# A two-layer graph kernel: the first graph's turn ahead of the score weights, the last graphs turned on TensorE, and both ends of the order placed anew

## The chip, the core and the metric

The kernel runs on one core of one Trainium2 chip. TensorE multiplies matrices, VectorE (DVE) and ScalarE (ACT) read its sums from PSUM, GpSimd (POOL) works on SBUF alone, and SyncE (SP) issues nearly all DMAs from one queue, in order. The metric is the device time of one execution in microseconds. Before the change the median of three runs is 2680.06 us (2679.51 to 2684.79).

## What is computed

128 graphs of 128 nodes with 512 features each pass two layers. Both have a layer norm and a ReLU ahead of them and add their result to the input. The first is graph attention with eight heads, the second a hypergraph convolution with a hidden size of 1024:

```python
h = relu(layernorm(x))
feats = einsum("nf,hfu->hnu", h, W)                      # per head, 64 units
dense = leaky_relu(e_self[:, None] + e_neigh[None, :]) + NEG_BIG * (1 - adj)
x = x + relu(softmax(dense) @ feats + b)                 # layer 0
h = relu(layernorm(x))
conv(v, W, b) = D^-1 H B^-1 H^T (v @ W^T) + b            # H = adj != 0
x = x + conv(layernorm(relu(conv(h, W1, b1))), W2, b2)   # layer 1
```

Everything is float32. `e_self` and `e_neigh` are the features times two vectors per head; the kernel folds these vectors into 16 extra columns of the first weight, the score weights.

## The kernel before

Work goes graph by graph, and two graphs make a pair. Of each graph there are steps with names: `x` loads, normalizes and turns (transposes) the input; `f` is the product with the first weight (eight matmuls, four to each of two PSUM banks, L583; the trace shows every matmul as two records, a transpose as one); `e` and `d` make the scores, which ACT, POOL, DVE and ACT again turn into exponentials `pp`; `p` turns them; `av` multiplies them with the features; `o` turns that result back; then the second norm `h` and the product `z` with the graph's own matrix `kk`. Of each pair there are the products `u1` to `u7` with W1 and `v1` to `v7` with W2, a seven-product scheme (four blocks of weights, two graphs; L830), between which DVE adds up the sums (`.keep` steps), the ReLU `r`, its turn (`ra.turn`, `rb.turn` for the first and second graph of the pair), and the last products `ya` and `yb`, after which `finish` (L947) adds the input and sends the result out.

A turn is done in one of two ways (`send` L481, `fetch` L490, `turn` L503). From the fifth graph on, SP writes the rows to DRAM, reads them back in four blocks, and DVE transposes 32x32 blocks. For the first four graphs (`DIRECT = 4`) nothing is sent: TensorE transposes 128x128 blocks, four to a PSUM bank, and DVE (first four blocks) or ACT (next four) copies them out. `blocks` (L475) says how the rows must lie for each way.

PSUM has eight banks. Two form the tile `pa` (first user: the rows of the score weights, then every `f` and half of every `d`), two rotate as `ps` (turns, `e`, `z`, `av`, `y`, biases), and four are named `ux`, `uy`, `vx`, `vy`, for the sums of the pairs' products; `uy` or `vy` also takes a part of `d`.

The order of all work is written out by hand. Every step has a place, a number in microseconds: its graph's origin (19.7 apart, the first eight listed in `EARLY`), plus the step's offset in `AT`, less a correction by group for the first eight graphs (`EARLY`) and the last ones (`LATE`). `put` (L990) works this out, and `Order.issue` sorts by place and issues; each engine then runs its instructions in that order, and waits at each for what it needs. So a place that changes moves a step only if it passes another one of the same engine.

At the start, TensorE spreads the rows `a_self` and `a_neigh` over 128 partitions (`score_rows`, L299, into `pa`); ACT copies the second to SBUF for POOL; DVE and POOL multiply both with the four blocks of the first weight and DVE sums up (`score_weights`, L305: three DVE instructions and one of POOL for each of four blocks). `bias_rows` (L326) spreads `b0`, `b1`, `b2`. `features` (L583) of graph 0 takes the score columns from the separate tile `we_sb`; `join_weights` (L323) copies them into the weight for later graphs.

Of the kernel before, what the change touches and what calls it, by code (L numbers as in the profile page):

```python
# [20 lines left out]
G = 2  # L21
STEP = 19.7
EARLY = (
    (0, 0, 4.32, -3.31, -3.04, -23.63, 1.9, -22.92, -47.35),
    (17.06, 1.25, -1.46, -0.55, 0, 0, -1.12, -1.26, -1.12),
    (36.56, 0, 0, -4.01, -4.09, 17.16, 19.45, 9.03, 5.36),
    (56.46, 0, 24.24, 0, 0.38, 0.45, -2.88, 0.44, 1.71),
    (76.16, 0, 0, 0, 0.74, -35.63, -3.58, -9.83, -12.38),
    (95.86, -1.88, 14.47, -1.29, 0, 0, 0, 0, 0.17),
    (115.56, -1.01, -1.01, -1.1, -1.57, -1, -6.4, -14.14, 11.79),  # L30
    (135.26, 0, 0.2, 0, 0.25, 0, 0, 0, -0.33),
)
LATE = (
    (0, 0.06, 0.98, 0, 13.88, 13.88, 5.19, 7.18),
    (0, -31.07, 0.07, 0.07, 0.26, 0.3, 0.26, -1.16),
    (0, 0, 0.62, 0.51, 4.26, 4.81, 4.81, 4.81),
    (0, 11.83, 0, -0.45, 0.41, -0.45, -0.45, 0.35),
)
AT = {
    "x.load": -21.95,  # L40
    "x.stats": -15.53,
    "x.rstd": -15.44,
    "x.relu": -11.99,
    "x.send": -10.85,
    "x.fetch": -7.73,
    "x.turn": -5.54,
    "f": 0,
    "f.keep": 3.07,
    "e": 3.9,
    "e.keep": 3.95,  # L50
    "d": 5.43,
    "d.leaky": 6.82,
    "d.mask": 8.25,
    "d.max": 12.88,
    "d.exp": 13.13,
    "d.exp1": 15.17,
    "p.send": 18.81,
    "p.fetch": 20.79,
    "p.turn": 26.62,
    "av": 29.32,  # L60
    "av.keep": 29.42,
    "o.send": 30.44,
    "o.fetch": 35.98,
    "o.turn": 37.55,
    "o.scale": 38.14,
    "o.add": 39.38,
    "h.stats": 42.94,
    "h.rstd": 43.02,
    "h.relu": 46.17,
    "z": 48.11,  # L70
    "z.keep": 51.23,
    "h.add": 51.08,
    "mask.load": -38.04,
    "mask": -24.21,
    "adj.load": -17.21,
    "adj.turn": 13.26,
    "adj.weigh": 17.47,
    "k": 31.92,
    "k.keep": 38.55,
    "us1": 55.31,  # L80
    "us2": 57.51,
    "us3": 55.61,
    "us4": 90.08,
    "u1": 62.8,
    "u1.keep": 70.95,
    "u6": 73.82,
    "u6.keep": 81.18,
    "u2": 76.53,
    "u2.keep": 78.64,
    "r.aL": 79.95,  # L90
    "u5": 84.05,
    "u7": 85.22,
    "u7.keep": 85.8,
    "r.bR": 88.18,
    "u4": 90.98,
    "u4.keep": 96.2,
    "r.bL": 96.27,
    "u3": 90.17,
    "u3.keep": 92.36,
    "r.aR": 96.53,  # L100
    "rb.send": 96.52,
    "rb.stats": 100.8,
    "ra.send": 99.31,
    "ra.stats": 103.65,
    "rb.fetch": 97.63,
    "rb.turn": 102.59,
    "ra.fetch": 101.73,
    "ra.turn": 113.63,
    "vs1": 112.91,
    "vs3": 117.27,  # L110
    "vs2": 120.49,
    "vs4": 137.15,
    "v1": 129.15,
    "v1.keep": 132.3,
    "a1": 133.14,
    "b1": 137.57,
    "b0": 137.67,
    "v6": 141.07,
    "v6.keep": 141.58,
    "v2": 136.71,  # L120
    "v2.keep": 138.79,
    "v5": 144.57,
    "v7": 142.41,
    "v7.keep": 145.53,
    "v4": 150.39,
    "v4.keep": 153.91,
    "v3": 150.01,
    "v3.keep": 151.98,
    "ya": 161.01,
    "ya.keep": 163.25,  # L130
    "yb": 178.91,
    "yb.keep": 183.24,
}
W2_AT = (43.52, -5.54, 3.84, 45.52, 47.16, 57.34, 58.49, 1.46, 76.99, 1.07, 11.58, 8.21)
DIRECT = 4


class Order:
# [4 lines left out]
        self.todo = []  # L143

    def at(self, place, fn, *args):
        self.todo.append((place, len(self.todo), fn, args))

    def issue(self):
        for _, _, fn, args in sorted(self.todo, key=lambda t: t[:2]):
# [4 lines left out]
def gat_then_hypergraph_kernel(  # L154
# [17 lines left out]
    N, C, F = x.shape  # L172
# [44 lines left out]
    def load_x(n):  # L217
        S[n]["xt"] = io.tile([P, F], F32, tag="xt", name=f"xt_{n}")
        nc.sync.dma_start(S[n]["xt"], x[n])
# [18 lines left out]

    load_x(0)
    S[0]["done"] = {"x.load"}
    t1, t2, t4 = (const.tile([P, KP, FV], F32, name=f"w2_t{i}") for i in (1, 2, 4))
    gb = const.tile([2 * KH, P], F32, name="gb")
    rows = {}
# [43 lines left out]
    bw_bc = const.tile([P, F], F32, name="bw_bc")  # L289
    cm = const.tile([P, F], F32, name="cm")  # L290
    gbT = const.tile([P, 2 * KH], F32, name="gbT")
    a_ps = psum2("a_bc")
    a_bc = [a_ps[:, t] for t in range(2)]
    an_bc = wk.tile([P, F], F32, tag="h1", name="an_bc", bufs=1)

    def spread(out, row):
# [175 lines left out]

    def blocks(n, rows):  # L475

        if n < DIRECT:
            return rows.rearrange("p (k b y) -> p k b y", b=NB, y=B)
        return rows.rearrange("p (b k y) -> p k b y", b=NB, y=B)

    def send(n, key, rows, k):  # L481

        S[n][key + "r"] = rows
        if n < DIRECT:
            return
        d = dr.tile([P, NB, k * B], F32, tag=key + "d", name=f"{key}d_{n}")
        S[n][key + "d"] = d
        nc.sync.dma_start(d, rows.rearrange("p (b c) -> p b c", b=NB))

    def fetch(n, key, k):  # L490
        if n < DIRECT:
            return
        d = S[n].pop(key + "d")
        m = wk.tile(
            [P, NB, k * B], F32, tag=key + "m", name=f"{key}m_{n}", bufs=1
        )
        S[n][key + "m"] = m
        for b in range(NB):
            nc.sync.dma_start(  # L499
                m[b * B : (b + 1) * B], d[:, b, :].rearrange("(a x) r -> x a r", x=B)  # L500
            )

    def turn(n, key, k, tag, bufs=2):  # L503
        rows = S[n].pop(key + "r")
        S[n][tag] = wk.tile([P, k, P], F32, tag=tag, name=f"{tag}_{n}", bufs=bufs)
        if n < DIRECT:
            for q in range(k // 4):
                t = psum(f"{key}t_{n}_{q}")
                for j in range(4):
                    at = (q * 4 + j) * P  # L510
                    nc.tensor.transpose(t[:, j * P : (j + 1) * P], rows[:, at : at + P], ident)
                half = S[n][tag][:, q * 4 : (q + 1) * 4, :].rearrange("p k c -> p (k c)")
                if q:
                    nc.scalar.copy(half, t)
                else:
                    nc.vector.tensor_copy(half, t)
            return
        nc.vector.transpose(  # L518
            S[n][tag].rearrange("p k (a x) -> p k a x", x=B),
            S[n].pop(key + "m").rearrange("p a (k y) -> p k a y", y=B),  # L520
        )
# [51 lines left out]
    def relu_x(n):  # L573
        s = S[n]
        s["xn"] = wk.tile([P, F], F32, tag="xn", name=f"xn_{n}", bufs=1)
        norm_relu(
            n,
            "a",
            blocks(n, s["xn"]),
            s["xt"].rearrange("p (k b y) -> p k b y", k=KF, y=B),  # L580
        )

# [98 lines left out]
    def exps(n, part):  # L681
        s = S[n]
        if part == 0:
            s["pp"] = wk.tile([P, H * P], F32, tag="pp", name=f"pp_{n}", bufs=1)
            s["rsum"] = sm.tile([P, H], F32, tag="rsum", name=f"rsum_{n}")
        nmx, sc = s["nmx"], s["sc"]
        for h in range(part * H // 2, (part + 1) * H // 2):
            nc.scalar.activation(  # L688
                blocks(n, s["pp"])[:, h],
                sc[:, h, :].rearrange("p (b y) -> p b y", y=B),  # L690
                AF.Exp,
                bias=nmx[:, h : h + 1],
                accum_out=s["rsum"][:, h : h + 1],
            )
# [17 lines left out]
    def keep_attention(n):  # L712
        s = S[n]
        s["oT"] = wk.tile([P, F], F32, tag="oT", name=f"oT_{n}", bufs=1)
        nc.scalar.activation(
            blocks(n, s["oT"]),
            s.pop("av").rearrange("p (k b y) -> p k b y", k=KF, y=B),
            AF.Relu,
        )
# [44 lines left out]
    def keep_hidden(n, q, hid):  # L764

        s = S[n]
        if "r" not in s:
            s["r"] = wk.tile([P, DH], F32, tag="r", name=f"r_{n}")
            s["sum"] = sm.tile([P, 2], F32, tag="sum", name=f"sum_{n}")
        nc.scalar.activation(  # L770
            blocks(n, s["r"])[:, q * 4 : (q + 1) * 4],
            hid.rearrange("p (k b y) -> p k b y", k=4, y=B),
            AF.Relu,
            accum_out=s["sum"][:, q : q + 1],
        )
# [186 lines left out]


    order = Order()
    order.at(-30, score_rows)
    for k in range(KF):
        order.at(-40 + k, load_w0, k)
        order.at(-12 + k, score_weights, k)
    order.at(-12, bias_rows, "b0", b0_bc)
    order.at(-30, load_mask, 0)  # L970
    order.at(0.5, join_weights)
    order.at(2, load_w1)
    order.at(W2_AT[0], load_w2)
    order.at(W2_AT[1], bias_rows, "b1", b1_bc)
    order.at(W2_AT[2], bias_rows, "b2", b2_bc)
# [168 lines left out]
    for n in range(N):  # L1144
        if n % G == 0:
            for group, key, fn in first:
                if n or key != "mask.load":
                    put(n, group, AT[key], fn, n // G)
        for group, key, fn in parts:
            if n or key != "x.load":  # L1150
                put(n, group, AT[key], staged, key, fn, n, S)
        if n % G == G - 1:
            for group, key, fn in second:
                put(n, group, AT[key], staged, key, fn, n // G, SP)
# [37 lines left out]
```

## Time and profile before

| | |
|---|---|
| median of three runs | 2680.06 us |
| the profiled execution | 2679.3 us |
| its span, first to last instruction | 2677.5 us |
| TensorE busy | 2612.1 us (98%) |
| VectorE, GpSimd, ScalarE busy | 1909.0, 1878.9, 1502.1 us |
| mean granted TensorE clock | 0.989 |

The profiled execution's own time is 1.8 us more than its span. In the views below a line of the timeline has the start, the time that it took, the engine, the source line, the operation, what it writes and reads, and in brackets the idle time of the engine before it with what ended it. A "PEld" line is a weight load of TensorE. A table by stretches gives, for each stretch of the span, its length and each engine's busy time.

### The profile page before, as it was taken

What the parts mean: (1) busy time and instruction counts of PE and PEld (TensorE: products, weight loads), DVE (VectorE), ACT (ScalarE), POOL (GpSimd) and SP (SyncE); (2) the same over time, 40 slices, a digit from 0 to 9 for tenths busy, and PEclk for the clock granted to TensorE, in tenths of its full rate; (3) what the DMA queues carried; (4) which work ended last, traced back from release to release, by engine and by line L of the source; (5) the groups of instructions that cost most, each with busy time, mean ns of one, the idle gap of its engine ahead of it and who ended that gap; (6) DMA issues with size and microseconds to landing.
All of it is one profiled execution on the core that took longest, in us unless ns stands there. A gap on an engine that the chain in (4) does not pass through costs nothing.

```text
span 2677.5 us, 42248 instructions
## 1 busy us (share of the span) xinstructions
PE 2612.1 (98%) x12433; PEld 1803.4 (67%) x12433; DVE 1909.0 (71%) x3554; ACT 1502.1 (56%) x4945; POOL 1878.9 (70%) x2196
## 2 busy tenths in 40 slices
PE   7799999999999999999999999999999999999998
PEld 4566666676666667667667667667666666667665
DVE  4566777777776777777777777777777677777763
ACT  3466556556556556656656556556556556555542
POOL 4667777777767777767767767777777777777762
PEclk8899999999999999999999999999999999999999
DMA  3246566566666566566666566666666666666632
GB/s 111 65 129 184 177 203 193 176 200 196 181 200 191 176 207 195 185 192 199 184 189 199 180 195 198 186 192 195 189 188 199 184 188 199 191 186 200 193 119 90
DMA packets 504496, 482.18 MB, mean 180 GB/s; under 512 B 136117, under 2 KB 406469, under 8 KB 504266
## 3 DMA queue, kind: packets, MB, share of 16 engines
q1 hardware_dynamic: 504256, 479.47, 59.4%
q8 instruction: 99, 1.62, 0.3%
q14 instruction: 131, 1.07, 0.1%
q10 hardware_dynamic: 10, 0.01, 0.0%
HBM read 250.70 MB, written 228.59 MB: 179 GB/s over the span
## 4 chain that ended last, share of the span: by engine, by line
PE 71%; DMA 11%; SPq 6%; DVE 5%; ACT 4%; issue 2%; POOL 1%; DVEq 0%; ACTq 0%; POOLq 0%
PE f L594 14%; PE uy L852 10%; PE vy L852 8%; PE vx L852 7%; PE uz L852 6%; PE vz L852 6%; PE ux L852 6%; SPq L499 5%; DMA pm<-pd 4%; PE av L704 4%; PE y L943 3%; PE z L744 3%; PE d L655 2%; DMA rd<-r 2%; DMA xm<-xd 2%
## 5 line engine op out<-in xcount | busy, mean ns | idle before, releaser
L594 PE MATMUL f<-w_sb,hT 128*128 128x264 f32 (+1 forms) x2048 | 485.8, 391 | 11.8 <-issue 6.6
L594 PEld LDWEIGHTS f<-w_sb,hT 128*128 128x128 f32 x2048 | 392.9, 193 | 109.3 <-issue 37.4
L688 ACT ACTIVATE pp<-sc,nmx 128x128 f32<-128x128 f32 x1024 | 397.4, 393 | 98.7 <-DVE nmx L679 98.7
L674 POOL TENSOR_TENSOR sc<-sc,at 128x1024 f32<-128x1024 f32 x128 | 303.2, 2368 | 65.6 <-ACT sc L669 65.6
L852 PE MATMUL vx<-w_sb,rT 128*128 128x256 f32 x1024 | 248.2, 385 | 1.0 <-ACT b L906 1.0
L852 PE MATMUL ux<-w_sb,zT 128*128 128x512 f32 x512 | 240.6, 592 | 0.0
L636 ACT COPY lt<-eT 128x128 f32<-128x128 f32 x128 | 34.1, 266 | 364.4 <-PE eT L628 364.4
L459 POOL TENSOR_SCALAR ve_a<-mv_a 128x1 f32<-128x1 f32 x128 | 28.3, 221 | 258.4 <-DVE mv_a L457 240.3
L852 PEld LDWEIGHTS vx<-w_sb,rT 128*128 128x128 f32 x1024 | 184.8, 190 | 34.2 <-issue 13.0
L730 POOL TENSOR_TENSOR xt<-xt,o 128x512 f32<-128x512 f32 x128 | 163.0, 1273 | 51.7 <-DVE o L726 49.8
L688 ACT ACTIVATION_READ_ACCUMULATOR pp<-sc,nmx 128x1 f32 x1024 | 195.9, 191 | 0.0
L518 DVE STREAM_TRANSPOSE pT<-pm 128x1024 f32<-128x1024 f32 x124 | 154.0, 1242 | 52.1 <-DMA pm<-pd 48.6
L787 ACT ACTIVATE sq<-r,nm 128x512 f32<-128x512 f32 x256 | 182.9, 715 | 4.2
L679 DVE TENSOR_REDUCE nmx<-sc 128x8 f32<-128x1024 f32 x128 | 155.4, 1214 | 35.2 <-POOL sc L674 35.0
L770 ACT ACTIVATE r<-aL 128x512 f32<-128x512 f32 x64 | 40.4, 632 | 237.0 <-DVE aL L863 237.0
L762 POOL TENSOR_TENSOR xt<-xt,b_bc 128x512 f32<-128x512 f32 x128 | 163.1, 1274 | 10.0
L828 POOL TENSOR_TENSOR rT<-rT,rT 128x512 f32<-128x512 f32 x64 | 82.0, 1281 | 125.3 <-DVE rT L518 108.3
L469 ACT ACTIVATE h<-xt,nmr_b,rstd_b 128x512 f32<-128x512 f32 x128 | 103.4, 808 | 115.6 <-POOL nmr_b L464 115.6
L761 POOL TENSOR_TENSOR xt<-xt,h 128x512 f32<-128x512 f32 x128 | 163.4, 1277 | 5.5 <-ACT h L469 5.3
L744 PEld LDWEIGHTS z<-kk,h 128*128 128x128 f32 x1024 | 134.2, 193 | 41.9 <-issue 27.4
L852 PEld LDWEIGHTS ux<-w_sb,zT 128*128 128x128 f32 x512 | 97.1, 190 | 94.6 <-issue 78.4
L518 DVE STREAM_TRANSPOSE rT<-rm 128x1024 f32<-128x1024 f32 x124 | 151.5, 1221 | 12.4 <-DMA rm<-rd 12.2
(163 smaller groups left out, 6358.3 us busy)
## 6 DMA issues: line engine op xcount, KB each, us to landing
pd<-pp SPq DMA_DIRECT2D x124, 512.0 KB, 3.7
pm<-pd SPq DMA_DIRECT2D x496, 128.0 KB, 3.7
rd<-r SPq DMA_DIRECT2D x124, 512.0 KB, 3.6
rm<-rd SPq DMA_DIRECT2D x496, 128.0 KB, 3.0
xt<-in_x SPq DMA_DIRECT2D x128, 256.0 KB, 3.0
out<-xt SPq DMA_DIRECT2D x128, 256.0 KB, 2.8
xd<-xn SPq DMA_DIRECT2D x124, 256.0 KB, 2.2
xm<-xd SPq DMA_DIRECT2D x496, 64.0 KB, 2.0
```

The source lines that it names most:

```text
L499: nc.sync.dma_start(m[b * B : (b + 1) * B], d[:, b, :].rearrange("(a x) r -> x a r", x=B))
L518: nc.vector.transpose(S[n][tag].rearrange("p k (a x) -> p k a x", x=B), S[n].pop(key + "m").rearrange("p a (k y) -> p k a y", y=B),)
L594: nc.tensor.matmul(s["f"][:, b, cols], hT[:, k, :], weights[:, k, b, :], start=(k == 0), stop=(k == KF - 1),)
L674: nc.gpsimd.tensor_tensor(s["sc"], s["sc"], neg.to_broadcast([P, H, P]), ALU.add)
L679: nc.vector.tensor_reduce(s["nmx"], s["sc"], AX.X, ALU.max, negate=True)
L688: nc.scalar.activation(blocks(n, s["pp"])[:, h], sc[:, h, :].rearrange("p (b y) -> p b y", y=B), AF.Exp, bias=nmx[:, h : h + 1], accum_out ...
L730: nc.gpsimd.tensor_tensor(s["xt"], s["xt"], s.pop("o").rearrange("p k c -> p (k c)"), ALU.add)
L744: nc.tensor.matmul(s["z"][:, k * P : (k + 1) * P], s["h1"][:, k * P : (k + 1) * P], SP[n // G]["kk"][:, n % G, :], start=True, stop=True,)
L761: nc.gpsimd.tensor_tensor(s["xt"], s["xt"], s["h1"], ALU.add)
L762: nc.gpsimd.tensor_tensor(s["xt"], s["xt"], b2_bc, ALU.add)
L787: nc.scalar.activation(sq, s["r"][:, q * 512 : (q + 1) * 512], AF.Square, bias=nm[:, 1:2], accum_out=ss[:, q : q + 1],)
L852: nc.tensor.matmul(p[w + bank][:, 0:cols], left[:, k, :], right[:, k, :], start=(first and k == 0), stop=(k == kb - 1), skip_group_check=n ...
```

## The change

The change has six parts.

1. The first graph's turn goes ahead of the score weights on DVE, and ahead of the bias rows on TensorE. Its norm goes ahead of the mask on POOL and ahead of the score rows' copy on ACT.
2. The two score rows are spread into the banks `ux` and `vx`, and no longer into `pa`.
3. The rows of `b2` are spread ahead of the first `f`, together with those of `b0` and `b1`. On SP, `x` of graphs 1 and 2 is loaded right after the first weight and mask; the second-layer weight W2 is loaded ahead of the third pair's mask.
4. The last graph's `p` and `o` turns (graph 127) and the last pair's `r` turns (graphs 126 and 127) are done on TensorE: 4 bank fills for `r`, 2 for `p`, 1 for `o`, each of four transposes and a copy.
5. The places of the first eight and now the last six graphs are set anew (`EARLY`, `LATE`).
6. Offsets in `AT` move a little. In every pair of the middle this passes other steps in four places: on TensorE `u6` goes ahead of `v3` and `v4`, and `v6` ahead of `yb`; on POOL `b1` goes ahead of `us2`, and `b0` behind `o.add`; on SP the mask load goes behind the fetch of `ra`. DVE and ACT keep their order in the middle.

At the ends, TensorE's order changes so: after graph 0, `e` 4 goes ahead of `u1` 0, `u6` 0 ahead of `z` 2, `u5` 1 ahead of `e` 7, `av` 6 ahead of `z` 5; in the last pairs `u6` stands ahead of `v3`, `yb` between `v6` and `v7`, the turn `rb` 63 between `v5` and `v3` of pair 62, `ya` 62 between `v1` and `v2` of pair 63. On DVE, `yb.keep` 61 and `v7.keep` 62 stand ahead of the turn `rb` 63, `yb.keep` 60 ahead of the turn `rb` 62, and `yb.keep` 59 and the turn of `p` 127 ahead of the turn `rb` 61. On SP `rb` and `ra` of pairs 61 and 62 are both sent before either is fetched. Counts of instructions in the middle do not change.

The core of the diff (the tables of numbers are cut to what is spoken of):

```diff
 LATE = (
-    (0, 0.06, 0.98, 0, 13.88, 13.88, 5.19, 7.18),
...
+    (0, 0, 0, 0, 0, 43.36, 50.78, 44.34),
+    (0, 0, 0, -1.28, 0, -2.85, 0, -0.14),
...
 )
 AT = {
...
-    "mask.load": -38.04,
-    "mask": -24.21,
+    "mask.load": -34.65,
+    "mask": -21.04,
...
-    "u6": 73.82,
+    "u6": 70.97,
...
-    "b1": 137.57,
-    "b0": 137.67,
+    "b1": 135.65,
+    "b0": 138.73,
...
-    "yb": 178.91,
-    "yb.keep": 183.24,
+    "yb": 180.67,
+    "yb.keep": 182.25,
 }
 DIRECT = 4
+LAST = {"x": 0, "p": 1, "o": 1, "r": 2}
...
-    load_x(0)
-    S[0]["done"] = {"x.load"}
...
-    a_ps = psum2("a_bc")
-    a_bc = [a_ps[:, t] for t in range(2)]
+    a_bc = [psum_sums(tag, f"a_bc_{tag}") for tag in ("ux", "vx")]
...
-    def blocks(n, rows):
+    def direct(n, key):
+        return n < DIRECT or n >= N - LAST[key]
+
+    def blocks(n, key, rows):
-        if n < DIRECT:
+        if direct(n, key):
             return rows.rearrange("p (k b y) -> p k b y", b=NB, y=B)
...
     def turn(n, key, k, tag, bufs=2):
...
-        if n < DIRECT:
+        if direct(n, key):
             for q in range(k // 4):
...
-    order.at(-30, score_rows)
+    order.at(W2_AT[12], score_rows)
     for k in range(KF):
-        order.at(-40 + k, load_w0, k)
-        order.at(-12 + k, score_weights, k)
-    order.at(-12, bias_rows, "b0", b0_bc)
-    order.at(-30, load_mask, 0)
+        order.at(-99 + k, load_w0, k)
+        order.at(W2_AT[13] + k * W2_AT[14], score_weights, k)
+    order.at(W2_AT[15], bias_rows, "b0", b0_bc)
+    order.at(-95, load_mask, 0)
+    order.at(W2_AT[16], adj_masks, 0)
     order.at(0.5, join_weights)
-    order.at(2, load_w1)
+    order.at(W2_AT[17], load_w1)
...
-            if n or key != "x.load":
+            if n < 3 and key == "x.load":
+                order.at(-100 + 6 * n, staged, key, fn, n, S)
+            else:
                 put(n, group, AT[key], staged, key, fn, n, S)
```

## The prediction

> **What bounds the kernel now.** I read the busy shares first, then the table by stretches, then TensorE's timeline at both ends. From the page:
>
> ```profile
> PE   7799999999999999999999999999999999999998
> ...
> PEclk8899999999999999999999999999999999999999
> ```
>
> TensorE is full but for the first three and the last of 40 slices, and only the first two slices show a lower clock. The table by stretches (start, end and length, then busy time of PE, PEld, DVE, ACT, POOL, then clock):
>
> ```profile
> 0.00:21.00 21.00, 9.99 (x15) 3.91 (x15) 10.71 (x28) 4.23 (x6) 7.85 (x16) 1.00 0.80 225
> 21.00:200.00 179.00, 152.21 (x708) 101.51 (x709) 99.48 (x202) 88.28 (x290) 112.98 (x117) 0.87 0.29 87
> 200.00:2560.00 2360.00, 2349.33 (x11331) 1631.56 (x11330) 1748.10 (x3247) 1374.35 (x4544) 1707.88 (x2006) 1.00 0.64 191
> 2560.00:2674.00 114.00, 100.55 (x382) 66.45 (x380) 50.24 (x81) 35.22 (x107) 50.18 (x59) 0.96 0.29 93
> ```
>
> The middle holds 2360 us and only 10.7 us (2360.00 less 2349.33) in which TensorE is idle: two `f` lie 39.74 us apart where nothing waits, 40.0 on average. The ends are small but loose: 11.0 us idle before the first `f` at 21 us, 26.8 to 200 us, 13.4 in the last 114. So what can be won lies at the ends; in the middle the change must only not lose. The start:
>
> ```profile
> 6.47 5.32 PE L297 MATMUL b<-w_t,ones 1*128 1x512 f32 x6
> 9.36 1.10 POOL L527 TENSOR_SCALAR at<-at 128x256 f32<-128x256 f32 x1 [7.98 <-DMA at<-in_adj]
> 13.27 1.08 PE L511 MATMUL xt<-ident,xn 128*128 128x128 f32 x4 [1.48 <-ACT b_bc L331]
> 18.99 1.28 DVE L314 TENSOR_REDUCE we_sb<-prod 128x8 f32<-128x512 f32 x2
> 20.19 0.68 DVE L516 COPY hT<-xt 128x512 f32<-128x512 f32 x1
> 20.97 5.88 PE L594 MATMUL f<-w_sb,hT 128*128 128x256 f32 x16 [6.61 <-issue]
> 28.47 1.12 PE L297 MATMUL b<-w_t,ones 1*128 1x512 f32 x2
> ```
>
> The reader sees graph 0's norm behind the mask on POOL (9.36), its turn on TensorE at 13.27, and the copy that `f` 0 needs (20.19) at the end of the score weights in DVE's queue. "issue" before `f` 0 is that copy. The end (TensorE):
>
> ```profile
> 2587.14 1.98 PE L704 MATMUL av<-pT,feats 128*64 128x128 f32 x16 [4.04 <-DVE pT L518]
> 2589.04 3.56 PE L852 MATMUL vz<-w_sb,rT 128*128 128x256 f32 x8
> ...
> 2620.89 1.97 PE L852 MATMUL vz<-w_sb,rT 128*128 128x256 f32 x8 [2.76 <-DVE v L915]
> ...
> 2642.98 1.99 PE L852 MATMUL vy<-w_sb,rT 128*128 128x256 f32 x8 [0.65 <-DVE a L915]
> ...
> 2649.71 3.22 PE L852 MATMUL vz<-w_sb,rT 128*128 128x256 f32 x8 [3.00 <-DVE v L915]
> ...
> 2658.65 1.99 PE L852 MATMUL vx<-w_sb,rT 128*128 128x256 f32 x8 [0.98 <-ACT b L906]
> ...
> 2663.87 1.99 PE L852 MATMUL vy<-w_sb,rT 128*128 128x256 f32 x8 [0.65 <-DVE a L915]
> ...
> 2668.26 1.97 PE L852 MATMUL vz<-w_sb,rT 128*128 128x256 f32 x8 [0.67 <-DVE v L915]
> ```
>
> `av` 127 waits for a turn through DRAM; `v3` of pairs 61 and 62 waits for `v7.keep`, which stands in DVE's queue behind the turn `rb`, itself waiting for a DMA. And two groups of eight take 3.56 and 3.22 us where the others take 1.97.
>
> **The Trainium skill.** "TensorE: Matmul & The Clock Gate", Part 1: the clock is halved by default and after a window of about 3.4 us without enough activity. The trace agrees: the clock is 0.50 from 2585.41 to 2592.23 and from 2650.26 to 2653.67, right after the two long stalls, and for 47.8 us in all between 32 and 148 us. Part 4 says that transposes don't count as activity; no stretch here shows it alone. "DMA: Bandwidth & Descriptors", Anatomy of one DMA: about 2 us fixed for each; here 2.0 to 3.7 us from issue to landing, twice for a turn. "PSUM — Partial Sum Buffer", on bank collisions: a bank must be guarded as a whole; so while `pa` holds the score rows, `f` 0 would have to wait for their last reader.
>
> **The start, step by step.** `x` 0 lands as before, its sums are ready at 4.46 us; without the mask ahead, POOL's three instructions (1.27 us at 10.54) end at 5.8, ACT's norm (0.81) at 6.6, just as TensorE ends the score rows (6.67). Four transposes (1.08): 7.8; copy (0.68): 8.5. The first weight is there by 8 us (the small packets of its eight DMAs end then). Now four bias spreads stand ahead of `f` 0, not three: 4 x 1.77 (5.32/3) = 7.1, so `f` 0 starts at 14.9, not 20.97. Its score columns need the score weights: DVE from 8.5, four times 2.05 (18.28 to 20.27 for one, say), 16.7; covered by `f` 0's main part (at 5.5 to 5.9 us to about 20.5), the columns (1.85) end at 22.3. Before, 28.54 plus 1.1 for `b2` (28.47), `e` 0 at 29.52; now `e` 0 at 22.5. Gain 7.0. The rest is pushed by `f` 0's end and follows: ACT now runs `e.keep` 0 ahead of graph 1's norm, 0.8 us, hidden while TensorE runs `d` 0 (0.71) and DVE the adjacency (1.6). W1 moves behind two loads of 256 KB; it ended by 17 to 18 us before, and POOL, who now takes a 2.35 us block of it ahead of the mask of scores, needs it at 19. The new banks alone save little: the last reader of the score rows would be done by 15.4, against 14.9.
>
> From graph 3 to 8 swaps on TensorE mostly fill one wait and open another, since DVE, ACT and POOL pace this part (`u6` 0 ahead of `z` 2 fills 1.43 us, but `f` 5 waits for DVE's turn anyway; `u1` 0 behind `e` 4 puts 1.0 us ahead of `d` 4, hidden by POOL's queue; `av` 6 may gain 1.9). I take 0, between -2.5 and +2.
>
> **The end, step by step.** Removed waits, all from the lines above: `av` 127 4.04; at `v3` 61 2.76 less what remains with `u6` (1.73 us) ahead of it and `v7.keep` still behind a DMA, 0.9, so 1.9; `v7` 62 0.65 (`yb`, 0.85, fills it); `v3` 62 3.00 (`v7.keep` no longer stands behind a turn); `v2` 63 0.9; `v3` 63 0.67. Sum 11.1. Added transposes: 28, at 0.5 us for four (groups of four take 0.42 to 0.66 when the clock is full): 3.6. Their seven copies lie on DVE and ACT, which are half idle there. Added waits: `z` 126 for a bank, 0.3; `u7` 62 for `u6.keep`, 0.4; `v1` 63 for the copy of `ra`, 0.25; and `z` 127. Its chain (copy `o`, scale, add, norm, ReLU) took 7.0 us before (2595.23 to 2602.27), just hidden; now `o` is turned earlier, but TensorE arrives 4.9 us earlier: 1.4 open. Sum 2.35. Behind `z` 127 stand `v1` 61 and everything later. The slow clock of 2585 to 2592 cost 0.9 (`av`, 1.98 against 1.10) and 1.6 (`v3`): 2.5, gone with the stall. That of 2650 cost 1.6; eight transposes stand there now, so I leave it in. Sum: -11.1 + 3.6 + 2.35 - 2.5 = -7.65.
>
> **The middle.** No instruction is added. `u6` needs `us2`, done 15 us earlier (1534.3 against about 1549.6), and a bank which ACT left 1.9 us before; `v3` and `v4`, 1.73 us later, are read by DVE 0.8 and 1.6 us after that. `b1` fills a POOL wait of 1.23 us. The mask load (0.40 us on SP) leaves a hole before the fetch of `ra` and now stands ahead of the sends of `y` and `x`; `x.send` waits for ACT anyway (1509.1), and `f` has 1.0 us of slack behind its turn. It also leaves the DMA engines to `p`'s fetch, whose turn causes most of the 10.7 us. I take 0, from -4 to +4.
>
> Sum: -7.0 + 0 - 7.65 + 0 = -14.7. Profiled execution 2679.3 - 14.7 = 2664.6; it lay 0.76 below the median of the runs, so the forecast is 2665.3.
>
> **Rivals.** *One end only* (the start's slow clock windows fall worse, or the transposes keep the clock down at the end and `z` 127 waits 3 us): -7 to -8, 2672.5. For it: 17 us of half clock between 80 and 97. *More*: the second slow window goes too (1.6), the middle's turns lose half their waits (4), graphs 4 to 8 gain 2: 2658. For it: the middle's stalls sit mostly on odd graphs, where the mask load was. *Slower*: the mask load holds `x.send` of odd graphs by 0.4 us, and that comes through to `f` in each of 60 pairs, +24, so 2665.3 + 24 = 2689. It decides once `hT` is late by more than the 1.0 us of slack; `f` waited in only a few odd graphs, by at most 1.05, which speaks against. *Nothing*: the start's gain is swallowed by the pace of DVE and POOL from graph 3 on, and the end's by cold transposes: 2679.
>
> **Chances.** Forecast 0.58, one end 0.17, more 0.13, slower 0.07, nothing 0.05. Range: the forecast's own 2661 to 2670, reaching to the cases beside it: 2656 to 2675. A measurement of this kernel tells about 0.2% (5.4 us) from no change. Faster by more 0.87, within 0.06, slower 0.07.
>
> **What would show it.** `f` 0 starts at 15 us, not 21, and `e` 0 at 22.5; `av` 127 waits under 0.5 us and has no half clock around it; `z` 127 waits 1 to 2 us; `v3` 62 doesn't wait; `f` to `f` stays at 39.74 per pair with about 11 us idle in the middle. The forecast is wrong if the middle's idle time grows beyond 15 us, or if the distance from `f` 0 to `f` 8 (150.4 us) grows by what the start won.

## The result, and the profile after

The changed kernel takes 2672.8 us (median of 20 runs, 2666.6 to 2679.3), the kernel before on the same chip 2680.9 (20 runs, 2677.2 to 2687.2). The ratio is 0.9965, 95% interval [0.9957, 0.9973]: 9.4 us faster by the ratio, 8.2 by the medians, where 14.7 had been forecast. The profiled execution took 2671.9 us, its span is 2670.1. The busy tenths of TensorE look as before but for the first slice (8 for 7) and the last (9 for 8):

```profile
PE   8799999999999999999999999999999999999999
...
PEclk8899999999999999999999999999999999999999
```

The table by stretches of the changed kernel (columns as in the prediction; the first stretch ends at 15 us, where `f` 0 now begins):

```profile
0.00:15.00 15.00, 9.95 (x14) 3.84 (x14) 4.81 (x18) 4.23 (x6) 6.14 (x15) 1.00 0.77 204
15.00:190.00 175.00, 142.59 (x668) 94.88 (x669) 98.01 (x196) 83.28 (x270) 108.95 (x115) 0.86 0.29 88
190.00:2550.00 2360.00, 2348.98 (x11336) 1631.44 (x11335) 1746.32 (x3244) 1374.82 (x4543) 1707.03 (x2005) 1.00 0.64 191
2550.00:2667.00 117.00, 104.49 (x398) 69.42 (x396) 56.94 (x94) 39.74 (x127) 56.77 (x64) 0.96 0.33 105
```

These four lines are those of the kernel before, cut at the new borders. The same cut of the changed kernel:

```profile
0.00:15.00 15.00, 11.96 (x17) 4.33 (x17) 9.12 (x26) 4.33 (x6) 7.84 (x16) 1.00 0.78 205
15.00:190.00 175.00, 146.73 (x706) 98.28 (x706) 99.74 (x203) 87.92 (x289) 111.81 (x117) 0.89 0.32 97
190.00:2550.00 2360.00, 2340.80 (x11284) 1621.68 (x11285) 1737.95 (x3226) 1365.81 (x4521) 1677.12 (x2000) 1.00 0.63 190
2550.00:2667.00 117.00, 111.60 (x464) 75.06 (x460) 60.12 (x102) 42.79 (x132) 58.69 (x65) 1.00 0.24 79
```

Three of the stretches got fuller: TensorE does more in the same time at the start, and the last stretch has full clock (1.00 for 0.96). The third got emptier: 19.2 us idle (2360.00 - 2340.80) where the kernel before had 11.0. That is where part of the gain went. TensorE's timeline at the start of the changed kernel:

```profile
6.79 1.12 PE L514 MATMUL xt<-ident,xn 128*128 128x128 f32 x4 [0.91 <-ACT xn L469]
7.83 7.19 PE L297 MATMUL b<-w_t,ones 1*128 1x512 f32 x8
14.96 6.53 PE L597 MATMUL f<-w_sb,hT 128*128 128x256 f32 x16
21.32 1.85 PE L597 MATMUL f<-we_sb,hT 128*128 128x8 f32 x16
23.52 0.41 PE L631 MATMUL eT<-ident,pad 128*128 128x128 f32 x2 [0.35 <-DVE pad L611]
```

`x` 0 is turned at 6.79 us (13.27 before), the spreads of the biases fill the time to 14.96, and `f` 0 follows with no wait. `f` 8 starts at 161.78 us, 9.6 sooner than before (171.41). The end:

```profile
2585.65 1.13 PE L747 MATMUL z<-kk,h 128*128 128x128 f32 x8 [0.44 <-DVE pT L519]
2586.71 1.09 PE L707 MATMUL av<-pT,feats 128*64 128x128 f32 x16
...
2589.55 1.89 PE L855 MATMUL vz<-w_sb,rT 128*128 128x256 f32 x8
...
2597.60 1.98 PE L855 MATMUL uz<-w_t,us 128*128 128x512 f32 x4 [1.42 <-DVE aL L866]
...
2601.69 1.16 PE L747 MATMUL z<-kk,h 128*128 128x128 f32 x8 [0.39 <-ACT h L469]
...
2643.31 1.92 PE L855 MATMUL vz<-w_sb,rT 128*128 128x256 f32 x8
...
2660.79 1.97 PE L855 MATMUL vz<-w_sb,rT 128*128 128x256 f32 x8 [0.67 <-DVE v L918]
```

`av` 127 (2586.71) no longer waits and takes 1.09 us for 1.98; the two slow groups of eight (3.56 and 3.22) take 1.89 and 1.92. A wait that was not foreseen stands at 2597.60. Followed step by step, the changed kernel is 9.6 us ahead of the kernel before at graph 8, 2.3 us behind it at 2540 to 2580 us, and 7.5 ahead at the last instruction. Both ends gave almost 10; what lies between, for which the forecast had 0, took 12 in this execution: 9.3 in graphs 8 to 119, whose order the experiments put back, and 2.5 from there to `f` 127. Which waits grew there, by group on TensorE from 200 to 2500 us (busy us and mean ns, then the idle time before the group), the kernel before first:

```profile
L594 PE MATMUL f<-w_sb,hT 128*128 128x264 f32 x1840 | 429.0, 386 | 2.6 <-DVE hT L518 2.4
...
L704 PE MATMUL av<-pT,feats 128*64 128x128 f32 x1840 | 125.8, 279 | 7.8 <-DVE pT L518 7.4
```

```profile
L597 PE MATMUL f<-w_sb,hT 128*128 128x264 f32 x1840 | 429.8, 387 | 7.0 <-DVE hT L521 6.8
...
L707 PE MATMUL av<-pT,feats 128*64 128x128 f32 x1824 | 124.7, 279 | 9.3 <-DVE pT L521 9.0
```

The times of the instructions are the same within 1 ns; the waits for the two turns through DRAM grew, `f`'s most. Of the 48 pairs of graphs 12 to 107, 18 keep the undisturbed 39.74 us, where 26 did.

### The profile page after: what moved, and what is told of

The parts are those of the page before. It is cut to its first block, busy times and chain, and to the rows that moved or that the text cites. A ratio compares the mean times of both kernels' runs of the same rounds, so it can differ in the third digit from the quotient of the medians.

```text
span 2670.1 us, 42320 instructions
## 1 busy us (share of the span) xinstructions
PE 2611.1 (98%) x12461; PEld 1799.3 (67%) x12461; DVE 1907.0 (71%) x3554; ACT 1500.8 (56%) x4948; POOL 1855.5 (69%) x2196
## 4 chain that ended last, share of the span: by engine, by line
PE 60%; DMA 17%; SPq 8%; DVE 7%; ACT 5%; issue 2%; POOL 1%; DVEq 0%; ACTq 0%; POOLq 0%
PE f L597 12%; PE uy L855 8%; SPq L502 7%; PE vy L855 7%; PE vx L855 6%; DMA pm<-pd 6%; PE uz L855 5%; PE ux L855 5%; PE vz L855 4%; DMA xd<-xn 3%; PE av L707 3%; PE y L946 3%; DMA pd<-pp 2%; DMA rd<-r 2%; PE z L747 2%
## 5 line engine op out<-in xcount | busy, mean ns | idle before, releaser
L521 DVE STREAM_TRANSPOSE hT<-xm 128x512 f32<-128x512 f32 x124 | 88.0, 710 | 114.7 <-DMA xm<-xd 114.6
L641 DVE TENSOR_TENSOR rt<-diag,eT 128x256 f32<-128x256 f32 x128 | 51.9, 405 | 153.6 <-ACT lt L639 153.6
```

The source lines that it names most:

```text
L521: nc.vector.transpose(S[n][tag].rearrange("p k (a x) -> p k a x", x=B), S[n].pop(key + "m").rearrange("p a (k y) -> p k a y", y=B),)
```

## The experiments

All but one have the changed kernel's code; a table `MID` replaces places of `AT` in graphs 8 to 119 alone, so that the ends keep their order. Each group of four ran on one chip, beside the kernel before; the three groups on three chips, so runs are compared within a group. Runs of different groups are compared only by their ratio to the kernel before beside them. Of each kernel one execution has a trace.

**First group: is it the order of the middle?** The kernel before took 2672.5 us here (25 runs).

```
 # old middle, new ends
+MID = {<all places of AT that differ>: <their values before>}
...
-                put(n, group, AT[key], staged, key, fn, n // G, SP)
+                put(n, group, when(key, n), staged, key, fn, n // G, SP)
```

> The changed kernel with the order of the kernel before in graphs 8 to 119 (mask load, u6, yb, b1 and b0 go back to their old places), both ends as changed. If the new order of the middle costs the 10 us that went missing: two ends of -9.7 us each and nothing lost, so 19 us below the kernel before, some 2661.5 us, and 39.99 to 40.02 us per pair of graphs. If the loss isn't the order of the middle but chance, or a phase that the new start sets: as the changed kernel, 9 us below the kernel before, 40.1 to 40.2 us per pair. As the forecast had it (middle 0, ends -14.7): 2666.

Measured: 2651.0 us (6 runs), ratio 0.9922 [0.9907, 0.9937]; 39.82 us per pair, 4.2 us idle between 200 and 2500 us. The two ends are worth 21.5 us here by the medians, and the old middle keeps it.

The reverse, the kernel before with the new values of `AT` in graphs 8 to 119 alone:

> The kernel before with the new order in graphs 8 to 119 alone. If the new order costs it: 7 to 10 us slower than the kernel before, some 2689 us, pairs at 40.15 us. If it is chance or the phase from the start: within 2 us of the kernel before. The forecast's middle: 0, from -4 to +4.

Measured: 2676.3 us (19 runs), ratio 1.0017 [1.0009, 1.0025], so 2.4 to 6.7 us slower. The new order of the middle costs time by itself, with the old start in front of it: it isn't chance, and it needs no phase that the new start sets. It is less than expected.

The start alone (old middle, old `LATE`, `LAST` all 0):

> The start of the changed kernel with the middle and the end of the kernel before. The forecast's step: -7.0 us; the trace of the changed kernel: -9.6 by graph 8. If the start's gain holds to the end: 2671 us, pairs at 40.0 us, and all the end's waits of before are back (13 us idle after 2500). If a phase set by the start costs the middle: 2679 to 2681.

Measured: 2660.9 us (5 runs), ratio 0.9961 [0.9948, 0.9974], -11.6 by the medians; TensorE waits 14.3 us after 2500, with `av` 127 waiting 4.36 and `v3` 62 3.02. So the end is worth 2660.9 - 2651.0 = 9.9 us. The start's share needs a second look. The 25 runs of the kernel before differ in their mean granted clock: the seven with 0.992 or more have a median of 2667.6 us, the sixteen with 0.990 or less 2674.0. With the new start the clock was 0.991 or 0.992 in all five runs. Against the runs of the higher clock the start gains 2667.6 - 2660.9 = 6.7 us, and both ends 2667.6 - 2651.0 = 16.6. The other 5 us go with the clock. Where in a run that lies is known of the traces alone: with the old start the two that there are have 47.8 us of half clock in the first 200 us (mean clock 0.989) and 41.0 (0.991, the run with the new middle alone), with the new start and `f` 0 at 15 us there are 37.5 to 41.0 in eleven.

The old bank for the score rows:

```
-    a_bc = [psum_sums(tag, f"a_bc_{tag}") for tag in ("ux", "vx")]
+    a_ps = psum2("a_bc")
+    a_bc = [a_ps[:, t] for t in range(2)]
```

> The changed kernel with the score rows back in a bank of the pair that f 0 uses; all else as changed. The forecast's working: the last reader of the score rows is done at about 15.4 us against 14.9 for f 0's start, so +0.5 us. If the bank is what the start's gain hangs on: f 0 begins behind the score weights, 18 us or later, +3 us or more, f 0 would be seen to wait for DVE.

Measured: 2658.9 us (5 runs), ratio 0.9951 [0.9937, 0.9964]. From DVE's timeline and TensorE's in this kernel:

```profile
14.17 0.68 DVE L311 TENSOR_TENSOR prod<-w_sb,a_bc 128x512 f32<-128x512 f32 x1
...
14.90 6.23 PE L600 MATMUL f<-w_sb,hT 128*128 128x256 f32 x16
```

The last product, the last reader of the score rows, ends at 14.85 us and `f` 0 starts at 14.90, with no wait; with the new banks on the same chip (old middle) it starts at 14.96. The bank is not what the start's gain hangs on, while four spreads stand ahead of `f` 0. On this chip the new middle cost 2658.9 - 2651.0 = 7.9 us if the bank is worth nothing.

**Second group: which part of the middle?** Kernel before 2675.6 us (9 runs); one part of the old order at a time is put back into the changed kernel.

```
 # one of
+MID = {"mask.load": -38.04, "mask": -24.21}
+MID = {"u6": 73.82, "yb": 178.91, "yb.keep": 183.24, "v6": 141.07, <v3, v4, v4.keep, u6.keep>}
+MID = {"b1": 137.57, "b0": 137.67}
```

> The changed kernel; in graphs 8 to 119 the mask load (and the instruction on it) goes back ahead of the fetch of ra on SP, the rest stays. If the mask's transfer beside the send and fetch of x is what costs the middle (theory 1): as the kernel with the whole old middle, 7 to 8 us below the changed kernel run beside it, and f waits for hT no more than 2 us in the middle. If it is TensorE's or POOL's order: as the changed kernel, within 2 us.

> The changed kernel with TensorE's order of before in graphs 8 to 119: u6 behind v3 and v4, yb and v6 in their old places. If u6 ahead of v3 and v4, and yb later, push what av and f wait for (theory 2): 7 to 8 us below the changed kernel. If the mask or POOL is the cause: within 2 us of it.

> The changed kernel with POOL's order of before in graphs 8 to 119: b1 behind us2 and vs4, b0 ahead of o.add. If b1 ahead of us2 costs it, because it holds us2 (0.9 to 1.0 us later in the changed kernel) that u6 now needs sooner (theory 3): 7 to 8 us below the changed kernel. If not: within 2 us, or 1 to 2 us above, since o.add now comes 1.1 to 1.3 us later again.

> The changed kernel itself, so that the three beside it have a yardstick on the same chip: 9 to 14 us below the kernel before. With the old bank for the score rows it was 13.6 below; if the bank is worth 0.5 us, 14 below on such a chip.

Measured, five runs each: the changed kernel 2658.6 us (2656.6 to 2663.0), ratio 0.9943 [0.9930, 0.9955]; the mask back 2654.1 (2651.1 to 2656.9), 0.9923 [0.9911, 0.9936]; TensorE's order back 2657.4 (2654.0 to 2658.3), 0.9937 [0.9924, 0.9951]; POOL's order back 2658.5, 0.9940 [0.9927, 0.9952]. POOL's swaps can't be told from nothing (theory 3 falls, also as a help), and neither can TensorE's 1.2 us. The mask load's place costs 4.5 us, the largest part, though less than the 7 to 8 that were expected of it. What it does is seen on SP. The issues of a pair with the mask load (`at`) in its new place (changed kernel), and in the old one:

```profile
1496.44 0.40 SPq L227 DMA_DIRECT2D at<-in_adj  x1
1496.94 0.41 SPq L961 DMA_DIRECT2D out<-xt  x1
1498.07 0.33 SPq L491 DMA_DIRECT2D xd<-xn  x1
1499.56 0.32 SPq L491 DMA_DIRECT2D od<-oT  x1
1500.58 1.74 SPq L502 DMA_DIRECT2D xm<-xd  x4
```

```profile
1490.64 0.40 SPq L229 DMA_DIRECT2D at<-in_adj  x1
...
1496.38 0.34 SPq L493 DMA_DIRECT2D xd<-xn  x1
1497.87 0.32 SPq L493 DMA_DIRECT2D od<-oT  x1
1498.42 1.76 SPq L504 DMA_DIRECT2D xm<-xd  x4
```

SP issues the fetch of `x` (`xm`) when the send (`xd`) has landed. With 128 KB of mask 1.6 us ahead of the send, 2.51 us lie between the two issues (1498.07 to 1500.58); with the mask 5.7 us ahead, 2.04. Over all odd graphs from 8 to 119 the medians are 2.65 and 2.40 us. SP's waits ahead of the fetch for the landing of the send, from 200 to 2500 us (us in total, times, longest), changed kernel and mask back, say the same:

```profile
SPq L502 <- DMA xd<-xn: 64.3, 67, 2.5
```

```profile
SPq L504 <- DMA xd<-xn: 36.2, 50, 2.7
```

How the later turn of `x` becomes lost time is less plain. TensorE's waits in the same two executions, changed kernel and mask back:

```profile
L597 PE MATMUL f<-w_sb,hT 128*128 128x264 f32 x1840 | 429.1, 386 | 3.7 <-DVE hT L521 3.3
...
L707 PE MATMUL av<-pT,feats 128*64 128x128 f32 x1840 | 125.8, 279 | 5.4 <-DVE pT L521 5.3
```

```profile
L599 PE MATMUL f<-w_sb,hT 128*128 128x264 f32 x1840 | 428.7, 386 | 3.3 <-DVE hT L523 3.3
...
L709 PE MATMUL av<-pT,feats 128*64 128x128 f32 x1840 | 125.8, 279 | 3.0 <-DVE pT L523 2.9
```

The wait for hT hardly fell (at most 2 us had been expected); the wait for pT did. One execution of each can't settle which of the two waits the mask load lengthens.

**Third group: SP's time or the transfer?** Old middle, new ends, and one load more per pair of graphs (56 pairs) into a tile that nobody reads. Kernel before 2679.8 us (19 runs).

```
+    def load_spare(g):
+        t = gp.tile([P, G, P], F32, tag="spare", name=f"spare_{g}", bufs=1)
+        nc.sync.dma_start(t[0:1, 0, 0:1], adj[g * G, 0:1, 0:1])  # 4 bytes; or the 128 KB of load_mask
...
+        if n % G == 0 and 8 <= n < N - 8:
+            put(n, X, -34.65, load_spare, n // G)  # at the old place: -38.03
```

> The kernel with the old middle and the changed ends, plus one load of 4 bytes per pair of graphs (into a tile that nobody reads) at the mask load's new place on SP. It takes SP's 0.4 us there without the traffic. If the mask's cost is SP's issue time in front of x's send (the prediction's slower rival): 4 us over the old middle, some 17 us below the kernel before. If it is the transfer: as the old middle, 21 us below the kernel before.

> As the run with 4 bytes, but the extra load is the mask's whole 128 KB (its own load stays at the old place). If the transfer beside x's send and fetch is the cost: 4 to 5 us over the run with 4 bytes, send to fetch of x in odd graphs 0.2 us longer, f waits more in odd graphs. If SP's issue is: the same as with 4 bytes.

> The extra 128 KB right beside the mask's own load at the old place: the control for the traffic as such. If the place is what counts: within 1 to 2 us of the run with 4 bytes. If any further 128 KB costs: the same as at the new place.

Measured: with 4 bytes 2659.8 us (6 runs), ratio 0.9920 [0.9903, 0.9937], what the old middle had without it on the first group's chip (0.9922); with 128 KB at the new place 2675.5 (14 runs), 0.9987 [0.9974, 0.9999]; with 128 KB at the old place 2666.3 (6 runs), 0.9944 [0.9928, 0.9959]. SP's issue (0.29 us for the 4 bytes, where the mask load takes 0.40) costs nothing that these ratios show, though their intervals are some 4.5 us wide to each side; the transfer costs 15.7 us at the new place and 6.5 at the old one. The control was expected to cost 1 to 2 us and cost 6.5: traffic costs in both places, but 9.2 us more at the new one, 0.16 us a pair (9.2/56). TensorE's groups from 200 to 2500 us with 4 bytes, with 128 KB at the new place, and at the old one:

```profile
L603 PE MATMUL f<-w_sb,hT 128*128 128x264 f32 x1840 | 428.7, 386 | 1.4 <-DVE hT L527 1.4
...
L713 PE MATMUL av<-pT,feats 128*64 128x128 f32 x1841 | 126.1, 279 | 7.8 <-DVE pT L527 7.5
```

```profile
L603 PE MATMUL f<-w_sb,hT 128*128 128x264 f32 x1824 | 426.0, 387 | 4.8 <-DVE hT L527 4.2
...
L713 PE MATMUL av<-pT,feats 128*64 128x128 f32 x1824 | 124.7, 279 | 16.1 <-DVE pT L527 15.6
```

```profile
L603 PE MATMUL f<-w_sb,hT 128*128 128x264 f32 x1840 | 429.3, 387 | 2.1 <-DVE hT L527 2.1
...
L713 PE MATMUL av<-pT,feats 128*64 128x128 f32 x1824 | 124.7, 279 | 14.2 <-DVE pT L527 13.7
```

Here the wait for hT comes with the new place (1.4, 4.8, 2.1), and the wait for pT with the traffic, wherever it lies (7.8, 16.1, 14.2). Between issue of the send and issue of the fetch of `x` in odd graphs lie 2.50, 3.13 and 2.92 us (medians of graphs 8 to 119). The new place is beside the send of the results (`out`) as well; which neighbour counts was not tried apart.

**A version meant to be faster than all.** In the same group:

```
-    order.at(W2_AT[1], bias_rows, "b1", b1_bc)
-    order.at(W2_AT[2], bias_rows, "b2", b2_bc)
+    order.at(60.2, bias_rows, "b1", b1_bc)
+    order.at(16.9, bias_rows, "b2", b2_bc)
```

> A version meant to be faster than all: old middle, changed ends, and of the four bias spreads ahead of f 0 the two of b1 go to just ahead of e 3 (a wait of 2.1 us) and that of b2 to just ahead of f 1. f 0 should start at 14.96 - 3 x 1.77 = 9.7 us; its score columns wait for DVE at about 16.7, so e 0 comes 4 us sooner; less 0.5 to 1 for b2 ahead of f 1: 3 us below the old middle, 24 us below the kernel before. If POOL and DVE pace the first graphs: as the old middle, 21 below.

Measured: 2658.6 us (2646.0 to 2660.1, 6 runs), ratio 0.9909 [0.9891, 0.9928].

```profile
9.77 5.77 PE L599 MATMUL f<-w_sb,hT 128*128 128x256 f32 x16
15.37 1.85 PE L599 MATMUL f<-we_sb,hT 128*128 128x8 f32 x16
17.48 0.44 PE L633 MATMUL eT<-ident,pad 128*128 128x128 f32 x2 [0.26 <-DVE pad L613]
```

`f` 0 comes where it was expected (9.77), `e` 0 sooner (at 17.5 for 23.2 in the run with 4 bytes, 5.7 us and not 4), `f` 8 at 156.3 us against 164.5 in that run. But the median is only 1.2 us below that run's, inside the scatter of both: whether the gain lasts isn't settled. The changed kernel itself did not run on this chip or the first group's; by the ratios to the kernel before (0.9909 here, 0.9922 in the first group, against 0.9943 and 0.9965) the two versions with the old middle are the faster ones.

## Why the prediction was right in its total and wrong in its middle

**The step that failed** is "The middle ... I take 0, from -4 to +4", and in it the sentence on the mask load: "`x.send` waits for ACT anyway (1509.1), and `f` has 1.0 us of slack behind its turn. It also leaves the DMA engines to `p`'s fetch". The first half holds: the send of `x` in odd graphs is still issued 0.03 us after ACT is done (median; over 0.3 us after in 3 of 56 graphs, none before), and an issue on SP at that place cost nothing that could be seen, as the load of 4 bytes shows. What counted was the 128 KB in flight: with them there, send to fetch of `x` takes longer, 2.51 us for 2.04 in the pair shown, and 2.86 for 2.53 in the median of the two kernels of the result. The 1.0 us of slack was about a median. In the odd graphs of 12 to 107 the turn of `x` ends 0.88 us before TensorE is free in the kernel before and 0.74 in the changed one (medians), and that alone would cost nothing; but it ended after TensorE was free in 4 of these 48 graphs before, and in 9 after. A stall needs only a few late ones. Nor did `p`'s fetch gain by it: the wait for pT rose from 7.8 to 9.3 us. The slower rival named the right place and the right sign, but another way (SP's queue) and too high a price: it is 0.08 us (4.5/56) to 0.16 us a pair and not 0.4. That the path goes through the late turns of `x` fits the result's two traces and the third group's; in the second group's two traces the time was lost ahead of `av`, so this last step isn't settled.

The mask explains 4.5 us of the changed kernel's loss on one chip, and a second 128 KB gives a difference of 9.2 between the two places on another. The loss of the whole middle was 4 to 8 us in the first group, and in the two traces of the result 9.3 in graphs 8 to 119. So what the rest of it is, some of which may be TensorE's swaps (1.2 us, not told from nothing), stays open.

**The start, -7.0**: the path was right. `f` 0 starts at 14.96 us (forecast 14.9); `e` 0 at 23.52 and not 22.5, since the main part of `f` 0 took 6.53 us and not 5.5 to 5.9 (why isn't shown). So the path gave 6.0 and not 7.0; from `f` 0 to `f` 8 another 3.6 came (146.8 us for 150.4), 9.6 in all in the trace. There was less half clock on the way, 37.5 us before 200 us where there were 47.8, and 0.89 for 0.86 in the table by stretches; 10.2 us of half clock in place of full are worth at most half of that, 5.1. The prediction left this out of its sum, though it had named it as a risk. That is the Trainium skill's clock gate ("TensorE: Matmul & The Clock Gate", Part 1), and this trace agrees with it in direction: less waiting (TensorE idle 31.3 us of the first 200, for 37.8), more clock. Why a given stretch is slow isn't shown. Against the first group's runs of the higher clock the start gains 6.7; that this is close to 7.0 is in part luck, since the path gave 6.0 and the rest was not forecast.

**The bank**: "save little" was right, `f` 0 at 14.90 us with the old one.

**The end, -7.65**: right in kind, 2 us short (9.7 in the trace, 9.9 by runs). Of the removed waits, all went but 0.67 at `v3` 63, and `v3` 61 kept 0.16 and not 0.9. The added ones: `z` 126 0.44 (0.3 forecast), `v1` 63 0.37 (0.25), `z` 127 0.39 (1.4), `u7` 62 none (0.4), and instead 1.42 at `u5` 62, which was not foreseen. It waits for DVE to read the bank of `u2` (`aL`), and in DVE's queue the turn of `o`, its reciprocal and its scale stand ahead of that in both kernels. Before, they were done at 2596.75, and `aL` still waited 1.11 us for `u2`. Now TensorE turns `o` behind `u2`, so that DVE's copy starts at 2595.36, when `aL` could run, and copy, reciprocal and scale (0.69, 0.19, 0.69) hold it up. That wait also gave `z` 127's chain the time that it was to be short of. Waits together: from 12.75 to 4.22 us, -8.5 (forecast -8.75). The transposes cost 3.05 (three times 0.87 for eight, 0.44 for four; forecast 3.6). And the second slow window, which the prediction left in, went with the stall ahead of it, transposes or not: slow clock is worth -4.3 in place of -2.5. Sum -9.8. Two slips of the prediction are small: its seven groups of transposes at 0.5 us make 3.5 and not 3.6, and the first slow window begins in the midst of the stall (2585.41; `av` 127 starts at 2587.14) and not right after it.

**Its own tests**: `av` 127 and `v3` 62 came as said, and two undisturbed `f` still lie 39.74 us apart, though fewer are undisturbed. `z` 127 waited 0.39 us and not 1 to 2. "The forecast is wrong if the middle's idle time grows beyond 15 us" came true (17.7 from 200 to 2500, where there were 10.6). So the total lies in the range partly by luck: both ends gave more than forecast in the trace and the middle took more. By its number, 2672.8, the result is that of the rival with one end only (2672.5), but not by what happened, since both ends gained.

## What to carry to other kernels

A DMA that is moved can cost in two ways: by the time on the queue that issues it, and by its bytes in flight beside the transfers around its new place. Test them apart with a load of a few bytes, and with a second copy of the whole load. Slack behind a DMA is to be read from its late tail and not from its median: the stalls come from the few that are late. And a long stall removed on TensorE can be worth slow clock as well: here 4.3 us beside 8.5 us of waits.

## What the runs showed of the hardware that was not expected

Not every stall of TensorE brings slow clock. Three of the traced kernels keep the old end (the kernel before, the new middle alone, the start alone). In them each of the six waits of 3.0 to 4.4 us near the end has a stretch of half clock with it, of 3.4 or 6.8 us, and none of the three waits of 2.3 to 2.8 us has. In the eleven traces with the new end, whose longest wait there is 1.42 us, there is no half clock from 2500 us up to TensorE's last instruction, although 28 transposes stand there.

The same change gains differently on different chips: 9.4 us in the result, 15.2 (a ratio of 0.9943) in the second group. The kernel before takes 2680.9 us beside the result and 2672.5, 2675.6 and 2679.8 in the three groups. With the old order of the middle TensorE was idle there for 4.2 us on one chip (two ends new) and for 10.1 on another (with 4 bytes more), but that is one execution each.

And one kernel's runs on one chip differ by 6 us with their mean granted clock: 2667.6 us at 0.992 or more and 2674.0 at 0.990 or less.
